# A graph network on one core: the order of the first loads, the block terms of edge places on GpSimd, and the block-end sums on ScalarE

## The chip, the cores and the metric

One core of one Trainium2 chip. A core has five instruction queues that run beside each other and wait for one another through semaphores: TensorE (PE, with its weight loads shown as PEld), VectorE (DVE), ScalarE (ACT), GpSimd (POOL) and SyncE (SP), which here only issues DMAs. Each queue runs its instructions in order. The metric is the device time of one execution in microseconds; lower is better.

## The reference

Four graph layers run one after the other on 3125 nodes with 128 features and 100,000 edges. Each takes `relu(layernorm(x))` and adds its result to x.

```python
h = relu(layernorm(x)); x = x + L0(h)   # two graph attention layers, 4 heads, softmax over a node's incoming edges
h = relu(layernorm(x)); x = x + L1(h)   # Lanczos steps: w = segment_sum(edge_weight * v[src], dst), three times, then 4 products
h = relu(layernorm(x)); x = x + L2(h)   # three mean-aggregating layers: segment_sum(h[src], dst) / degree, two products each
h = relu(layernorm(x)); x = x + L3(h)   # relu(msg_W @ [x[src], type embedding]) summed by dst, a product, layer norm
```

The edges come sorted by destination. `edge_weight` and `edge_type_16` are one number each per edge.

## The kernel before

Nodes are cut into 25 blocks of 128 (`NB`, `P`). The kernel turns the edge list into dense 128 x 128 adjacency blocks once and then works with matrix products. The stages that matter here are these.

*Places* (`place_edges`). Edges are laid out as 112 rows of 896 (`A`, `EC`). Raw fields arrive by DMA: `raw_dst`, `raw_edge_weight` and `raw_dst_next` on SP's queue, `raw_src` and `raw_edge_type` on ScalarE's. VectorE computes the destination block `db`, the source block `sb` and its pair, then counts in 13 masked sums (L989) what an edge row carries over to the next one (`carry`, L998). ScalarE splits the weights into three bf16 parts and copies transposed fields into `rec`. Then, in two parts (`HALVES`: 512 and 384 of the 896 columns), VectorE computes for each edge

- block terms that depend only on `db` and `sb`: `cap`, how many slots the block has, and `base`, where they begin (L1037 to L1048);
- its rank among the edges of the same pair of blocks, in 13 rounds of mask, scan and predicated copy (L1053 to L1056);
- from both, the place: lane, level, and an index into a table (L1060 to L1088).

GpSimd scatters the records into that table in DRAM with 782 indirect DMAs (L1096), one for each 128 edges, in the order `ORDER`, which begins at the edges of block 5. The table is filled with -1 before (`none`, L961). VectorE then tests that the edges of each block end where the program expects (`ENDS`, `LOW`): 25 compare-and-sum passes over `db` (L1107), a matrix product that sums over rows, and two small compares for each block (L1115, L1117). The result goes into `bad`, which decides at the very end whether a general version has to run instead.

*Layer 0's preparation* (`graph_and_layer0`): layer norm of x, projections, attention factors, and three bf16 parts of the scaled features (L1229 to L1328). x itself is loaded on SP's queue at the very start (L114, L115), since its DMA waits for nothing.

*Blocks and attention.* For groups of blocks (5 to 8, 9 to 12, ..., 21 to 24, then 0 to 2 and 3 to 4), `build_block` loads the block's slots from the table (L1167), which waits for all scatters that can hold its edges, turns keys with TensorE (L1173), makes one-hot matrices on VectorE (L1190, L1192), and multiplies them into the block's counts and weights (L1204, L1207). `attend` then runs the group's attention (L1365, L1379). Slots and keys have one buffer each, so the slots of a block are loaded while the block ahead of it is built.

A scheduler of the programming layer fixes the order of each queue at build time from program order, dependences and its own costs. A tile that is written again must first have been read by all its earlier readers; this holds across engines. The pool of `place_edges` is reused by layer 0's preparation.

Of the kernel before, what the change touches and what calls it, by code (L numbers as in the profile page):

```python
# [7 lines left out]
F32 = mybir.dt.float32  # L8
# [4 lines left out]
AF = mybir.ActivationFunctionType  # L13
OP = mybir.AluOpType
# [4 lines left out]
P = 128  # L19
N = 3125  # L20
NB = 25
# [30 lines left out]
EC = 896  # L52
# [848 lines left out]
class FastGnn(Gnn):  # L901
# [24 lines left out]
    def place_edges(self, placed):  # L926
# [9 lines left out]
        with ExitStack() as s:  # L936
# [14 lines left out]
            for name, dt, fill, skip, queue in loads:  # L951
# [2 lines left out]
                v = a[name[:3] if skip else name]  # L954
                queue.dma_start(t[:whole, :], v[skip : skip + whole * EC].rearrange("(p c) -> p c", c=EC))
                queue.dma_start(t[whole:, : rest - skip], v[whole * EC + skip :][None, :])
            nc.gpsimd.memset(rec, 0.0)
            per = BASE[NB] // P
            none = work.tile([P, 14 * ROOM], BF16, name="none")
            nc.gpsimd.memset(none, -1.0)  # L960
            nc.sync.dma_start(self.table[: BASE[NB]].rearrange("(p i r) f -> p i (r f)", p=P, r=14),  # L961
                              bc(none[:, None, :], [P, per // 14, 14 * ROOM]))
            number = tile("number")
# [31 lines left out]
            ps = psum.tile([P, P], F32, name="ps_small")  # L995
            nc.tensor.matmul(ps[:A, :n_pair], lhsT=before, rhs=tail, start=True, stop=True)
            carry = work.tile([A, n_pair], F32, name="carry")
            V.tensor_copy(carry, ps[:A, :n_pair])  # L998

            w = raw["edge_weight"]  # L1000
            parts = [tile(f"w16_{i}", BF16) for i in range(3)]
# [15 lines left out]
            for q, n in HALVES:  # L1017
                for f, t in fields:
                    ps = psum2.tile([P, 4, A], BF16, name="ps_rec")
                    for j in range(n):  # L1020
# [7 lines left out]
            names = (("cap", F32), ("base", F32), ("step", F32), ("rank", F32), ("r_i", I32), ("hi_i", I32), ("lane_f", F32),  # L1028
                     ("level_f", F32))
            t_cap, t_base, t_step, t_rank, t_r, t_hi, t_lane, t_level = (tile(m, dt) for m, dt in names)  # L1030
            idx = {}
            for i, (q0, n0) in enumerate(HALVES):
                lo, hi = q0 * P, (q0 + n0) * P
                cut = lambda t: t[:, lo:hi]

                cap, base, step, of_db = cut(t_cap), cut(t_base), cut(t_step), cut(db)
                V.tensor_scalar(cap, of_db, 24.0, 8.0, op0=OP.is_gt, op1=OP.mult)  # L1037
                V.tensor_scalar(cap, cap, 1.0, None, op0=OP.add)
                V.tensor_scalar(base, of_db, float(N_SLOTS[-1]), None, op0=OP.mult)
                for d in range(NB - 1):  # L1040
                    for _ in range(CAP[d] - CAP[d + 1]):
                        V.scalar_tensor_tensor(cap, of_db, d + 0.5, cap, op0=OP.is_lt, op1=OP.add)
                    more = N_SLOTS[d] - N_SLOTS[d + 1]
                    if more:
                        V.tensor_scalar(step, of_db, d + 1.0, float(more), op0=OP.min, op1=OP.mult)
                        V.tensor_add(base, base, step)
                V.tensor_tensor(step, cut(sb), cap, op=OP.mult)
                V.tensor_add(base, base, step)  # L1048
                rank = cut(t_rank)
                V.memset(rank, 1.0)  # L1050
                for b in range(n_pair):
                    mask = hot.tile([A, 4 * P], F32, name="mask4")[:, : hi - lo]
                    V.scalar_tensor_tensor(mask, cut(pair), float(b), cut(unit), op0=OP.is_equal, op1=OP.mult)  # L1053
                    run = hot.tile([A, 4 * P], F32, name="run4")[:, : hi - lo]
# [24 lines left out]
                nc.tensor.matmul(ps[:, :3], lhsT=self.ones[:A], rhs=wrong, start=True, stop=True)  # L1079
                V.tensor_reduce(self.bad[:, 2:3], ps[:, :3], axis=AX.X, op=OP.add)  # L1080
                V.copy_predicated(lane, bc(self.bad[:A, 2:3].bitcast(I32), [A, hi - lo]), cut(number))


                of = placed.tile([P, n0, A], I32, name=f"idx{i}")
                ps = psum2.tile([P, 4, A], F32, name="ps_idx")
                for j in range(n0):
                    nc.tensor.transpose(ps[:, j, :], t_lane[:, lo + j * P : lo + (j + 1) * P], self.ident[:A, :A])
                V.tensor_copy(of, ps[:, :n0])  # L1088
                for j in range(n0):
                    idx[q0 + j] = of[:, j]  # L1090
# [10 lines left out]
                self.placed[c] = st.ins  # L1101


            left = t_level
            sums = work.tile([A, NB], F32, name="sums")
            for d in range(NB):
                V.tensor_scalar(left, db, d + 0.5, None, op0=OP.is_lt, op1=OP.add, accum_out=sums[:, d : d + 1])  # L1107
            ps = psum.tile([P, P], F32, name="ps_small")
            nc.tensor.matmul(ps[:, :NB], lhsT=self.ones[:A], rhs=sums, start=True, stop=True)
            upto = work.tile([P, NB], F32, name="upto")  # L1110
            V.tensor_copy(upto, ps[:, :NB])
            beyond = work.tile([P, 2, NB], F32, name="beyond")
            V.memset(beyond, 0.0)
            for d in range(NB):
                V.tensor_scalar(beyond[:, 0, d : d + 1], upto[:, d : d + 1], float(ENDS[d] * P), None, op0=OP.is_gt)  # L1115
                if d:
                    V.tensor_scalar(beyond[:, 1, d : d + 1], upto[:, d - 1 : d], float(LOW[d] * P), None, op0=OP.is_lt)  # L1117
            V.tensor_reduce(self.bad[:, :1], beyond.rearrange("p i d -> p (i d)"), axis=AX.X, op=OP.add)


# [287 lines left out]
    def graph_and_layer0(self, counts, node):  # L1408
# [3 lines left out]
        with ExitStack() as s:  # L1412
            one = s.enter_context(tc.tile_pool(name="l0", bufs=1))
            self.open_attention(one)
            with ExitStack() as s2:
                tmp = s2.enter_context(tc.tile_pool(name="gat_h", bufs=1))
                two = s2.enter_context(tc.tile_pool(name="gat_r", bufs=2))
                psum = s2.enter_context(tc.tile_pool(name="gat_h_ps", bufs=3, space=PSUM))
                super().load_x()
                for i in (1, 2):  # L1420
                    self.attention_weights(tmp, i)
                for g in range(GN):
# [612 lines left out]
```

## Time and profile before

| | us |
|---|---|
| median of 3 runs | 3201.25 (3200.83 to 3203.47) |
| profiled execution, device time | 3195.56 |
| its span | 3193.8 |
| busy: PE, DVE, POOL, ACT | 2561.2, 2296.6, 1445.2, 917.4 |
| raw_dst lands, VectorE starts on it | 28.48 |
| first scatter (POOL L1096) | 108.30 |
| ends test starts, layer norm starts (DVE L1107, L1229) | 141.74, 174.97 |
| first one-hot of block 5 (DVE L1190) | 239.23 |

Times in the lower rows count from the start of the span. In a row of the timeline the first number is the start, the second the duration in us, then engine, line of the source, operation, output tile <- input tiles, shapes, count, and in brackets how long the engine sat idle before and what released it. "SPq" is a DMA issue on SP's queue; its duration is the time that the queue needed to issue it, not that of the transfer.

### The profile page before, as it was taken

What the parts mean: (1) busy time and instruction counts of PE and PEld (TensorE: products, weight loads), DVE (VectorE), ACT (ScalarE), POOL (GpSimd) and SP (SyncE); (2) the same over time, 40 slices, a digit from 0 to 9 for tenths busy, and PEclk for the clock granted to TensorE, in tenths of its full rate; (3) what the DMA queues carried; (4) which work ended last, traced back from release to release, by engine and by line L of the source; (5) the groups of instructions that cost most, each with busy time, mean ns of one, the idle gap of its engine ahead of it and who ended that gap; (6) DMA issues with size and microseconds to landing.
All of it is one profiled execution on the core that took longest, in us unless ns stands there. A gap on an engine that the chain in (4) does not pass through costs nothing. (4 is left out here: it accounts for less than half of the span.)

```text
span 3193.8 us, 52069 instructions
## 1 busy us (share of the span) xinstructions
PE 2561.2 (80%) x20788; PEld 1825.5 (57%) x20788; DVE 2296.6 (72%) x4015; ACT 917.4 (29%) x1785; POOL 1445.2 (45%) x1394
## 2 busy tenths in 40 slices
PE   0018787878787788798886999997999976989898
PEld 0017464646455655477675444445555546888897
DVE  7979999999989899899997010405455575666766
ACT  3035050505140212476665000002120212333333
POOL 1577777777777700055553000000120106777775
PEclk9979999999999999899999999998999997999999
DMA  6013130303131101000002878781000004444443
GB/s 187 14 18 98 25 98 20 98 20 101 31 94 28 51 32 62 1 2 1 1 1 80 298 272 302 273 301 45 1 1 1 5 18 138 130 139 133 128 131 85
DMA packets 127742, 276.54 MB, mean 87 GB/s; under 512 B 28645, under 2 KB 68468, under 8 KB 116532
## 3 DMA queue, kind: packets, MB, share of 16 engines
q1 hardware_dynamic: 62982, 198.30, 18.9%
q0 software_dynamic: 37856, 32.76, 4.8%
q10 hardware_dynamic: 26652, 42.05, 3.7%
q8 instruction: 165, 2.70, 0.4%
q14 instruction: 87, 0.71, 0.1%
HBM read 210.00 MB, written 63.02 MB: 85 GB/s over the span
## 5 line engine op out<-in xcount | busy, mean ns | idle before, releaser
L1096 POOL DMA_INDIRECT table<-rec,idx x782 | 773.6, 989 | 336.7 <-issue 237.4
L1365 DVE SCALAR_TENSOR_TENSOR over<-ps_row,minus,counts 128x512 bf16<-128x512 f32 (+3 forms) x1040 | 699.3, 748 | 15.9 <-ACT row L1483 12.0
L1379 PE MATMUL ps_acc<-parts,over 128*128 128x198 bf16 x5000 | 571.4, 251 | 134.1 <-POOL over L1362 34.7
L1379 PEld LDWEIGHTS <-over 128*128 128x128 bf16 x5000 | 391.8, 98 | 309.7 <-DVE over L1365 231.9
L1910 POOL DMA_INDIRECT m_far<-pre,src x401 | 397.8, 992 | 259.1 <-DVE skips L923 137.2
L1207 PE MATMUL ps_cw<-oh_w,oh_d 128*128 128x128 bf16 x4050 | 385.9, 224 | 56.7 <-DVE oh_w L1192 52.1
L1533 PE MATMUL ps_sum<-g,node 128*128 128x512 f32 (+1 forms) x1050 | 413.2, 552 | 12.9 <-DMA g<-weights 12.9
L1362 POOL TENSOR_TENSOR over<-above,counts 128x640 bf16<-128x640 bf16 x160 | 211.3, 1329 | 392.0 <-ACT above L1360 265.2
L1207 PEld LDWEIGHTS <-oh_d 128*128 128x128 bf16 x4050 | 303.8, 100 | 90.9 <-issue 68.7
L1204 PE MATMUL ps_cw<-oh_d,oh_s 128*128 128x128 bf16 x1350 | 299.0, 224 | 48.2 <-ACT w_out L1212 24.7
L1722 PE MATMUL ps_agg<-l_parts,counts 128*128 128x384 bf16 (+1 forms) x1875 | 317.3, 327 | 14.0 <-POOL l_parts L923 14.0
L1192 DVE TENSOR_TENSOR oh_w<-oh_s,keys 128x1024 bf16<-128x1024 bf16 (+2 forms) x561 | 325.4, 633 | 0.0
L1533 PEld LDWEIGHTS ps_sum<-g,node 128*128 128x128 f32 x1050 | 189.8, 192 | 222.1 <-issue 208.4
L1722 PEld LDWEIGHTS <-counts 128*128 128x128 fp8e4 x1875 | 183.5, 98 | 134.5 <-issue 11.3
L1754 POOL IOTA of_i<- 96x1 int32 x1 | 0.1, 135 | 480.2 <-PE ps_sum L1609 480.2
L1211 ACT ACTIVATE counts<-ps_cw 128x256 fp8e4<-128x256 f32 (+1 forms) x325 | 122.7, 378 | 303.9 <-PE ps_cw L1207 294.4
L1931 PE MATMUL agg_far<-m_far,oh_far 128*128 128x128 f32 x1246 | 173.8, 287 | 11.6 <-ACT m_far L1917 7.1
L1892 PE MATMUL agg_wide<-m_wide,oh_wide 128*128 128x128 f32 x1100 | 160.3, 289 | 26.5 <-ACT m_wide L1889 17.9
L1204 PEld LDWEIGHTS <-oh_s 128*128 128x128 bf16 x1350 | 133.6, 100 | 80.9 <-issue 49.9
L1347 PEld LDWEIGHTS <-counts 128*128 128x128 fp8e4 x1250 | 112.1, 98 | 102.3 <-ACT counts L1211 19.9
L1885 PE MATMUL ps_m<-skips,src_hot 128*128 128x128 bf16 x1650 | 159.3, 224 | 9.1 <-DVE src_hot L1875 9.1
L1931 PEld LDWEIGHTS agg_far<-m_far,oh_far 128*128 128x128 f32 x1246 | 156.6, 199 | 13.6 <-ACT m_far L1917 9.0
(353 smaller groups left out, 3532.1 us busy)
## 6 DMA issues: line engine op xcount, KB each, us to landing
g<-weights SPq DMA_DIRECT2D x75, 1024.0 KB
g<-weights SPq DMA_DIRECT2D x75, 576.0 KB
weights<-w_out ACTq DMA_DIRECT2D x150, 256.0 KB
src_row<-wide SPq DMA_DIRECT2D x32, 512.0 KB
table<-rec,idx POOLq DMA_INDIRECT x782
type_row<-wide SPq DMA_DIRECT2D x32, 384.0 KB
table<-none SPq DMA_DIRECT2D x1, 10864.0 KB
type_row<-types SPq DMA_DIRECT2D x25, 384.0 KB
```

The source lines that it names most:

```text
L1096: st = nc.gpsimd.indirect_dma_start(out=self.table, out_offset=bass.IndirectOffsetOnAxis(ap=idx[k][:, p : p + 1], axis=0), in_=rec[:, (k * ...
L1192: nc.vector.tensor_tensor(oh_w[:, t, :h], oh_s[:, :h], key(WT + t), op=OP.mult)
L1204: nc.tensor.matmul(ps[:, 0, j, :], lhsT=oh_s[of], rhs=oh_d[of], start=(j == c == 0), stop=last, skip_group_check=True)
L1207: nc.tensor.matmul(ps[:, 1, j, :], lhsT=oh_d[of], rhs=oh_w[:, t][of], start=False, stop=(last and t == 2), skip_group_check=True)
L1362: nc.gpsimd.tensor_tensor(over[:, : n * P], above, self.counts[:, sb, cols], op=OP.mult)
L1365: V.scalar_tensor_tensor(over[:, : n * P], row, minus[:, sb, i : i + 1], self.counts[:, sb, cols], op0=OP.is_gt, op1=OP.mult)
L1379: nc.tensor.matmul(banks[j // 2][:, j % 2, : 3 * F2], lhsT=over[:, j * P : (j + 1) * P], rhs=parts[:, sb, i].rearrange("p s f -> p (s f)") ...
L1533: nc.tensor.matmul(ps[:, c0 // 512, :m], lhsT=node[:, b, :], rhs=g[:, c0 - lo : c0 - lo + m], start=(b == 0), stop=(b == NB - 1))
L1722: nc.tensor.matmul(ps[:, :n], lhsT=self.counts[:, sb, db * P : (db + 1) * P], rhs=parts[:, sb, :n], start=(sb == 0), stop=(sb == NB - 1))
L1892: nc.tensor.matmul(agg, lhsT=oh[:, j, :], rhs=m[:, j, :], start=(x == 0), stop=(x == n_slots - 1))
L1910: nc.gpsimd.indirect_dma_start(out=m[:, j, :], out_offset=None, in_=pre, in_offset=bass.IndirectOffsetOnAxis(ap=src_of[:, a + j : a + j + ...
L1931: nc.tensor.matmul(agg[d], lhsT=oh[:, c - lo, :], rhs=m[:, c - a, :], start=(c == LOW[d]), stop=(c == ENDS[d] - 1))
```

## The change

There are three edits, and one reordering of two memsets.

- Loads: x is no longer loaded at the head of SP's queue but after the edge loads, the table fill and `types`; its DMAs also wait for the carry (`self.begun`). The memset of `none`, the source of the table fill, moves ahead of that of `rec`.
- Block terms: `cap` and `base` of both parts are computed on GpSimd ahead of the rank rounds. The fused compare-and-add of VectorE becomes a tensor_scalar and a tensor_tensor, 42 instructions in all, and a step of `CAP` by 4 is one pair instead of four fused ones.
- Ends test: ScalarE sums sign(2d + 1 - 2 db) over all edges for each block d, and VectorE compares the 25 sums with prepared limits in two instructions.

```diff
-            nc.gpsimd.memset(rec, 0.0)
             per = BASE[NB] // P
             none = work.tile([P, 14 * ROOM], BF16, name="none")
             nc.gpsimd.memset(none, -1.0)
+            nc.gpsimd.memset(rec, 0.0)
...
-            V.tensor_copy(carry, ps[:A, :n_pair])
+            self.begun = V.tensor_copy(carry, ps[:A, :n_pair]).ins
...
+            G = nc.gpsimd
+            for q0, n0 in HALVES:
+                cut = lambda t: t[:, q0 * P : (q0 + n0) * P]
+                cap, base, step, of_db = cut(t_cap), cut(t_base), cut(t_step), cut(db)
+                G.tensor_scalar(base, of_db, float(N_SLOTS[-1]), None, op0=OP.mult)
+                G.tensor_scalar(cap, of_db, 24.0, 8.0, op0=OP.is_gt, op1=OP.mult)
+                for d in range(NB - 1):
+                    more = N_SLOTS[d] - N_SLOTS[d + 1]
+                    if more:
+                        G.tensor_scalar(step, of_db, d + 1.0, float(more), op0=OP.min, op1=OP.mult)
+                        G.tensor_tensor(base, base, step, op=OP.add)
+                    if CAP[d] > CAP[d + 1]:
+                        G.tensor_scalar(step, of_db, d + 0.5, float(CAP[d] - CAP[d + 1]), op0=OP.is_lt, op1=OP.mult)
+                        G.tensor_tensor(cap, cap, step, op=OP.add)
+                G.tensor_scalar(cap, cap, 1.0, None, op0=OP.add)
+                G.tensor_tensor(step, cut(sb), cap, op=OP.mult)
+                G.tensor_tensor(base, base, step, op=OP.add)
...
-                V.tensor_scalar(cap, of_db, 24.0, 8.0, op0=OP.is_gt, op1=OP.mult)
-                V.tensor_scalar(cap, cap, 1.0, None, op0=OP.add)
-                V.tensor_scalar(base, of_db, float(N_SLOTS[-1]), None, op0=OP.mult)
-                for d in range(NB - 1):
-                    for _ in range(CAP[d] - CAP[d + 1]):
-                        V.scalar_tensor_tensor(cap, of_db, d + 0.5, cap, op0=OP.is_lt, op1=OP.add)
-                    more = N_SLOTS[d] - N_SLOTS[d + 1]
-                    if more:
-                        V.tensor_scalar(step, of_db, d + 1.0, float(more), op0=OP.min, op1=OP.mult)
-                        V.tensor_add(base, base, step)
-                V.tensor_tensor(step, cut(sb), cap, op=OP.mult)
-                V.tensor_add(base, base, step)
...
+            odd = work.tile([P, NB], F32, name="odd")
+            nc.gpsimd.iota(odd, pattern=[[2, NB]], base=1, channel_multiplier=0, allow_small_or_imprecise_dtypes=True)
+            limit = work.tile([P, 2, NB], F32, name="limit")
+            V.memset(limit[:, 1], -float(A * EC))
+            for d in range(NB):
+                V.memset(limit[:, 0, d : d + 1], float(2 * ENDS[d] * P - A * EC))
+                if d:
+                    V.memset(limit[:, 1, d - 1 : d], float(2 * LOW[d] * P - A * EC))
             sums = work.tile([A, NB], F32, name="sums")
             for d in range(NB):
-                V.tensor_scalar(left, db, d + 0.5, None, op0=OP.is_lt, op1=OP.add, accum_out=sums[:, d : d + 1])
+                nc.scalar.activation(t_level, db, AF.Sign, bias=odd[:A, d : d + 1], scale=-2.0, accum_out=sums[:, d : d + 1])
             ps = psum.tile([P, P], F32, name="ps_small")
             nc.tensor.matmul(ps[:, :NB], lhsT=self.ones[:A], rhs=sums, start=True, stop=True)
-            upto = work.tile([P, NB], F32, name="upto")
-            V.tensor_copy(upto, ps[:, :NB])
             beyond = work.tile([P, 2, NB], F32, name="beyond")
-            V.memset(beyond, 0.0)
-            for d in range(NB):
-                V.tensor_scalar(beyond[:, 0, d : d + 1], upto[:, d : d + 1], float(ENDS[d] * P), None, op0=OP.is_gt)
-                if d:
-                    V.tensor_scalar(beyond[:, 1, d : d + 1], upto[:, d - 1 : d], float(LOW[d] * P), None, op0=OP.is_lt)
+            V.tensor_tensor(beyond[:, 0], ps[:, :NB], limit[:, 0], op=OP.is_gt)
+            V.tensor_tensor(beyond[:, 1], ps[:, :NB], limit[:, 1], op=OP.is_lt)
...
-                super().load_x()
+                nc.vector.memset(self.x[:, NB - 1, :], 0.0)
+                x = self.a["x"]
+                for ld in (nc.sync.dma_start(self.x[:, : NB - 1, :], x[: (NB - 1) * P, :].rearrange("(b p) f -> p b f", p=P)),
+                           nc.sync.dma_start(self.x[:TAIL, NB - 1, :], x[(NB - 1) * P :, :])):
+                    self.wait_for(ld.ins, self.begun)
```

In the changed kernel's line numbers, the carry copy is L999, the rank rounds are L1059 to L1062, the Sign sums L1120, the two compares L1124 and L1125, and the scatter L1102. The tile `level_f` (`t_level`), which the sums use as their unread output, is also the tile in which VectorE forms the level of each place.

More of the change, by code (lines that the diff above doesn't have):

```diff
@@ L1034, in place_edges @@
                 cut = lambda t: t[:, lo:hi]
-                cap, base, step, of_db = cut(t_cap), cut(t_base), cut(t_step), cut(db)
-                V.tensor_scalar(cap, of_db, 24.0, 8.0, op0=OP.is_gt, op1=OP.mult)
-                V.tensor_scalar(cap, cap, 1.0, None, op0=OP.add)
-                V.tensor_scalar(base, of_db, float(N_SLOTS[-1]), None, op0=OP.mult)
-                for d in range(NB - 1):
-                    for _ in range(CAP[d] - CAP[d + 1]):
-                        V.scalar_tensor_tensor(cap, of_db, d + 0.5, cap, op0=OP.is_lt, op1=OP.add)
-                    more = N_SLOTS[d] - N_SLOTS[d + 1]
-                    if more:
-                        V.tensor_scalar(step, of_db, d + 1.0, float(more), op0=OP.min, op1=OP.mult)
-                        V.tensor_add(base, base, step)
-                V.tensor_tensor(step, cut(sb), cap, op=OP.mult)
-                V.tensor_add(base, base, step)
+                cap, base = cut(t_cap), cut(t_base)
                 rank = cut(t_rank)
@@ L1101, in place_edges @@
                 self.placed[c] = st.ins
-            left = t_level
+            odd = work.tile([P, NB], F32, name="odd")
[6 more added lines that the diff above has]
+                    V.memset(limit[:, 1, d - 1 : d], float(2 * LOW[d] * P - A * EC))
             sums = work.tile([A, NB], F32, name="sums")
             for d in range(NB):
-                V.tensor_scalar(left, db, d + 0.5, None, op0=OP.is_lt, op1=OP.add, accum_out=sums[:, d : d + 1])
+                nc.scalar.activation(t_level, db, AF.Sign, bias=odd[:A, d : d + 1], scale=-2.0, accum_out=sums[:, d : d + 1])
             ps = psum.tile([P, P], F32, name="ps_small")
             nc.tensor.matmul(ps[:, :NB], lhsT=self.ones[:A], rhs=sums, start=True, stop=True)
-            upto = work.tile([P, NB], F32, name="upto")
-            V.tensor_copy(upto, ps[:, :NB])
             beyond = work.tile([P, 2, NB], F32, name="beyond")
-            V.memset(beyond, 0.0)
-            for d in range(NB):
-                V.tensor_scalar(beyond[:, 0, d : d + 1], upto[:, d : d + 1], float(ENDS[d] * P), None, op0=OP.is_gt)
-                if d:
-                    V.tensor_scalar(beyond[:, 1, d : d + 1], upto[:, d - 1 : d], float(LOW[d] * P), None, op0=OP.is_lt)
+            V.tensor_tensor(beyond[:, 0], ps[:, :NB], limit[:, 0], op=OP.is_gt)
+            V.tensor_tensor(beyond[:, 1], ps[:, :NB], limit[:, 1], op=OP.is_lt)
             V.tensor_reduce(self.bad[:, :1], beyond.rearrange("p i d -> p (i d)"), axis=AX.X, op=OP.add)
```

## The prediction

> **What bounds the kernel now.** I read the page's engine rows first, then the waits, then the first 300 us in order of time, then busy time by stretch. The part that the change touches runs up to the first adjacency block, and beyond it the waits tell who passes a shift on.
>
> ```profile
> span 3193.8 us, 52069 instructions
> PE 2561.2 (80%) x20788; PEld 1825.5 (57%) x20788; DVE 2296.6 (72%) x4015; ACT 917.4 (29%) x1785; POOL 1445.2 (45%) x1394
> 51.80:108.30 56.50, 5.71 (x36) 3.90 (x36) 54.81 (x95) 20.01 (x25) 0.00 (x0) 1.00 0.21 66
> 141.70:175.00 33.30, 4.58 (x19) 3.42 (x19) 31.59 (x105) 3.30 (x4) 25.38 (x27) 1.00 0.11 31
> 233.00:1262.00 1029.00, 822.07 (x8558) 589.51 (x8558) 964.59 (x1678) 287.89 (x732) 675.74 (x694) 0.96 0.19 58
> ```
>
> The last three rows are stretches: length, then busy us of PE, PEld, DVE, ACT, POOL, then clock, DMA share, GB/s. VectorE is full while places are computed (54.81 of 56.50), full during the ends test, and 94% busy from 233 to 1262 us (blocks and layer 0's first attention). It is the bound from 28.5 us to 1262 us, so what moves its start there moves the end, unless the scatter becomes the later one. GpSimd is empty until the first scatter.
>
> ```profile
> 12.00:13.00 1.00, 0.00 (x0) 0.00 (x0) 0.00 (x0) 0.00 (x0) 0.00 (x0) 1.00 0.19 66
> ...
> 2.89 10.23 SPq L115 DMA_DIRECT2D x<-in_x_dram  x1
> 13.17 3.35 SPq L955 DMA_DIRECT2D raw_dst<-in_dst_dram  x1
> ...
> 28.48 0.63 DVE L968 TENSOR_SCALAR db_i<-raw_dst 112x896 int32<-112x896 int32 x1 [18.75 <-DMA raw_dst<-in_dst_dram]
> 35.08 1.09 DVE L921 TENSOR_TENSOR rest<-raw_edge_weight,w 112x896 f32<-112x896 f32 x1
> 108.30 1.26 POOL L1096 DMA_INDIRECT table<-rec,idx  x1 [98.65 <-DVE cap L1042]
> 141.74 1.08 DVE L1107 TENSOR_SCALAR_CACHE_REDUCE level_f<-db 112x896 f32<-112x896 f32 x1
> 291.43 0.27 SPq L1167 DMA_DIRECT2D slots<-table  x1
> 301.65 0.69 DVE L1190 TENSOR_TENSOR oh_s<-lane,keys 128x1024 bf16<-128x1024 bf16 x1 [1.32 <-PE keys L1173]
> ```
>
> Here x sits on SP's queue ahead of raw_dst, which VectorE awaits for 18.75 us. From 12 us the edge loads run at a DMA share of 0.19, three of 16 engines, about 70 GB/s. The last two rows belong to block 8: its slots are requested at 291.43, used at 301.65.
>
> **The change, part by part.** Zero is the start of the span.
>
> *Loads.* Moving x behind removes it from those three engines. ScalarE sees raw_dst, raw_edge_weight and raw_dst_next at 28.42, 33.55 and 38.82, so one 388.5 KB load alone takes about 5.2 us. First bytes move at 3 us. raw_src (ACT queue) and raw_dst (SP queue) will then share the three engines: 3 + 2 x 5.2, landing near 14.5. Type and weight share next, weight near 25, raw_dst_next near 30. VectorE starts 14 us earlier, but its seventh full-width step, L921, needs the weights and their ScalarE cast (0.94): 26.1 instead of 35.1. Gain: 9.0. The table fill moves up with them (its `none` memset of 0.46 no longer waits behind `rec`'s 5.33), and ends near 62 on the same three engines; the first scatter is far later, so it costs nothing. x now waits on SP for the carry (L999), behind types, whose issue stood 30.76 us[...]. It lands near 70; its reader, L1229, comes at 170. What is queued behind it (src_of, dst_of, the weights) is wanted later still. So zero, with 100 us of cover.
>
> *Block terms off VectorE.* Per half: base and cap (2), the add of 1, seven compare-adds, four min-multiplies, four adds, two closing operations. By the distance between starts (0.34 and 0.60 for 512, 0.27 and 0.47 for 384 elements) that is 10.2 us for the first half and 7.9 for the second. One stall of 1.6 us at 53.9 (of_i, behind ScalarE) is covered by then, too.
>
> *The same on GpSimd.* 22 tensor_scalar and 20 tensor_tensor. The nearest tensor_tensor row is L921 on POOL, 640 f32 in 1.36 us undisturbed, 2.13 ns an element: 10 x (512 + 384) x 2.13 = 19 us. No tensor_scalar of GpSimd is in the trace. Bounds: a free one-stream instruction (memset of rec, 0.85 ns; iota of number, 1.08 ns an element), and the two-input rate 2.13. "GPSIMD Engine Reference" (Engine selection) of the Trainium skill puts one-input operations near line rate, so I take 1.06: 11 x 896 x 1.06 = 10 us; at 2.13 it is 21. Sum 29 us (28 to 40). GpSimd starts when db is ready, near 17.5, and would be done long before the 108 us of its scatter. By busy shares this is free. A row speaks against it:
>
> ```profile
> 2281.76 2.18 POOL L1704 TENSOR_TENSOR skips<-skips,l_own 128x640 f32<-128x640 f32 x1 [24.94 <-DVE inv_col L1727]
> ...
> 2282.46 1.63 DVE L1730 SCALAR_TENSOR_TENSOR l_own<-agg_t,inv_col,l_own 128x128 f32<-128x128 f32 x1
> 2284.72 0.35 DVE L1730 SCALAR_TENSOR_TENSOR l_own<-agg_t,inv_col,l_own 128x128 f32<-128x128 f32 x1
> ```
>
> The same VectorE operation takes 0.35 alone and 1.63 while GpSimd adds 640 f32: it stood still for nearly all of GpSimd's 1.36. The Trainium skill says so as a rule ("SBUF — State Buffer", Who interferes with whom): the shared port pair is an exclusive lock, and a VectorE instruction with two SBUF inputs is fully blocked by a GpSimd one that reads SBUF; so is a one-input f32 one in a 2-port mode. Nearly all of VectorE's work here is such (masks, scans, predicated copies). So GpSimd's time is not beside VectorE's but inserted in it. By busy shares the sum below would end at -25; by row and rule, P is added to it. P is GpSimd's 29 us less what runs while VectorE waits anyway (17.5 to 26.1, less 3.4 us of its own work, about 6): P = 23, between 17 and 33.
>
> *Ends test.* Gone: 25 sums of 1.13 us on L1107, then 49 small compares; 174.97 - 141.74 = 33.2 us, with some idx work between. New: 25 Sign activations, whose output tile level_f is still read by VectorE's last lane step (start 140.65), so they can't start before it, though their input is ready at 17. Each: a cast of 896 took 0.94, Sign with a bias tile took 0.82 for 640 against 0.74 for a plain activation, and an accumulator read adds about 0.09: 1.16 with the wait. 25 x 1.16, four in_order copies that stand between (3.1), start 0.7, matmul and compares 1.4: 34.2 us. VectorE's queue holds L1124 ahead of the layer norm, so it waits. From 140.65 to 174.97 were 34.3. Worth nothing either way, between -3 and +4. The 50 memsets of `limit` (0.06 each) come before any load has landed.
>
> *Sums.* First scatter: -9.0 - 10.2 - 1.6 + 1.8 (more of the second half's rounds stand before it) + P = 4 us later, at 112. VectorE's norm: -9.0 - 18.1 - 1.6 + P = 6 us earlier. So the scatter is what is late next. Block 8 needs the first 133 scatters; the 133rd issues at 289.0, its slots load at 291.43, and 4.7 us from load to transposes (233.13 to 237.84 for block 5) make 296.1; the transposes stand at 301.1. Slack 5.0. Scatters slowed to 1.85 us while VectorE scans become fewer, 1 us back. The end then moves by the later of VectorE (-6) and scatter (4 - 1 - 5 = -2): about 4 us of VectorE's gain goes into a new wait for the slots of block 8. In general, end = P - 25. Later blocks have tens of us of slack (block 9's slots come 65 us before use), and the chain after 1262 us is unchanged, so it passes on one to one.
>
> The profiled execution took 3195.56 (span 3193.8), 5.7 below the median 3201.25. I apply the shift of -2 to the median: 3199.
>
> **Rivals.**
> A. The lock costs less than the row says: GpSimd fits between VectorE's instructions, P near 0 to 15. For it: VectorE did not slow when scatters ran beside its scans, GpSimd did (1.54 against 0.97). Against it: the row above. End -10 to -25, 3176 to 3191.
> B. Slower: GpSimd's tensor_scalar at the two-input rate or with more overhead, P of 31 or more. Place: masks and first scans, then the first scatter at 121 or later, and VectorE waiting at block 8. It decides from P = 31.4, where P - 25 passes 6.4 us (0.2%). At 2.13 ns P is about 32, +7; with 0.15 us more for each of 42 operations, +13: 3208 to 3214. For it: two-operation compares are not plain streams. Against it: the memset and iota rates.
> C. The loads do not come early: queues issue in another order and weights land at 29. Then +3 on either.
>
> **How the numbers follow.** 0.2% is about what a measurement of this kernel tells from no change, 6.4 us. Main case (P 18 to 31), 0.45: -7 to +6, of which 0.12 faster, 0.28 same, 0.05 slower. A, 0.27: 0.26 faster, 0.01 same. B with C, 0.28: 0.25 slower, 0.03 same. Faster 0.38, same 0.32, slower 0.30. The main case's own range is 3194 to 3207; with both signs likely, the range reaches to most of A and B: 3179 to 3212.
>
> **What would show it.** Right: raw_dst landing near 14.5, L921 near 26; L989 masks of 1.09 stretched to about 1.6 to 2.1 while GpSimd works; first scatter at 110 to 115; VectorE idle some 34 us ahead of L1124; a wait for PE keys of several us before block 8. Wrong: masks at 1.09 with the first scatter near 90 (A); GpSimd's tensor_scalar above 1 us for 512 elements and the first scatter beyond 120 (B); Sign activations that start before the last lane step.

## The result, and the profile after

| | before | changed |
|---|---|---|
| median on the same chip, 20 runs each, us | 3201.25 (3195.09 to 3208.02) | 3208.19 (3200.32 to 3214.38) |
| ratio, 95% interval | 1 | 1.0017 (1.001 to 1.0023) |
| span of the profiled execution, us | 3193.8 | 3206.5 |
| VectorE's L921; first scatter | 35.08; 108.30 | 23.74; 112.20 |
| layer norm of x starts | 174.97 | 167.41 |
| 159th scatter done (the last that block 9 needs) | 323.1 | 324.3 |
| first one-hot of block 9 | 392.99 | 394.61 |

The ratio of 1.0017 is 5.4 us (the medians lie 6.9 us apart): a small loss where I had forecast a gain of 2. The page of the changed kernel begins:

```profile
span 3206.5 us, 52074 instructions
PE 2568.5 (80%) x20788; PEld 1831.3 (57%) x20788; DVE 2275.1 (71%) x3926; ACT 943.4 (29%) x1835; POOL 1516.8 (47%) x1437
```

VectorE has 21.5 us less to do, GpSimd 71.6 and ScalarE 26 more. The same stretches as before:

```profile
51.80:112.20 60.40, 4.81 (x31) 3.23 (x28) 60.32 (x68) 14.77 (x20) 44.16 (x28) 1.00 0.14 40
134.90:167.40 32.50, 4.79 (x20) 3.34 (x20) 2.00 (x7) 30.44 (x54) 24.68 (x26) 1.00 0.11 31
225.00:1263.00 1038.00, 823.80 (x8557) 592.22 (x8557) 964.44 (x1676) 287.54 (x732) 676.09 (x702) 0.95 0.19 57
3.00:8.00 5.00, 0.00 (x0) 0.00 (x0) 5.00 (x4) 0.00 (x0) 5.00 (x3) 1.00 0.19 69
8.00:12.00 4.00, 0.00 (x0) 0.00 (x0) 1.71 (x4) 0.00 (x0) 1.62 (x2) 1.00 0.20 80
12.00:13.00 1.00, 0.00 (x0) 0.00 (x0) 0.63 (x1) 0.90 (x1) 0.00 (x0) 1.00 0.90 316
```

Until the first scatter VectorE is as full as before, with fewer instructions, and GpSimd is busy beside it. During the ends test ScalarE is full and VectorE empty. The edge loads come first: from 3 to 12 us they run at a share of 0.19 to 0.20, no faster than before, only earlier. In the 0.90 of 12 to 13 us the table fill is running beside them. In order of time:

```profile
1.72 0.25 SPq L955 DMA_DIRECT2D raw_dst<-in_dst_dram  x1
...
12.17 0.63 DVE L968 TENSOR_SCALAR db_i<-raw_dst 112x896 int32<-112x896 int32 x1 [2.47 <-DMA raw_dst<-in_dst_dram]
16.91 0.63 DVE L968 TENSOR_SCALAR sb_i<-raw_src 112x896 int32<-112x896 int32 x1 [4.12 <-DMA raw_src<-in_src_dram]
...
23.74 1.49 DVE L921 TENSOR_TENSOR rest<-raw_edge_weight,w 112x896 f32<-112x896 f32 x1
...
112.20 1.98 POOL L1102 DMA_INDIRECT table<-rec,idx  x1 [15.20 <-issue]
...
134.91 1.04 ACT L1120 ACTIVATE level_f<-db,odd 112x896 f32<-112x896 f32 x1 [39.74 <-DVE lane_f L1079]
...
166.70 0.18 DVE L1124 TENSOR_TENSOR beyond<-ps_small,limit 128x25 f32<-128x25 f32 x1 [29.20 <-PE ps_small L1122]
...
298.53 0.69 DVE L1198 TENSOR_TENSOR oh_s<-lane,keys 128x1024 bf16<-128x1024 bf16 x1 [6.69 <-PE keys L1181]
```

The last row is block 8, whose one-hots began at 301.65 before: 3.1 us earlier. Block 5 had been 8.5 us earlier (230.76 against 239.23); the rest went into block 8's wait of 6.69 us. At block 9 nothing of the gain is left. TensorE between 322 and 336 us, first before, then changed (a row is a run of like instructions):

```profile
326.24 2.00 PE L1379 MATMUL ps_acc<-parts,over 128*128 128x198 bf16 x20
328.71 0.48 PE L1173 MATMUL keys<-ident,slots 50*128 50x50 bf16 x5 [0.47 <-DMA slots<-table]
329.12 5.04 PE L1379 MATMUL ps_acc<-parts,over 128*128 128x198 bf16 x36
```

```profile
323.70 2.00 PE L1387 MATMUL ps_acc<-parts,over 128*128 128x198 bf16 x20
330.44 0.51 PE L1181 MATMUL keys<-ident,slots 50*128 50x50 bf16 x5 [4.74 <-DMA slots<-table]
330.89 5.31 PE L1387 MATMUL ps_acc<-parts,over 128*128 128x198 bf16 x34
```

The five transposes of block 9's keys stand in TensorE's queue between the 20th and the 21st of these products of the first group's attention (blocks 5 to 8). TensorE is at them 2.5 us earlier than before (325.70 against 328.24) and then waits 4.74 us for slots that were requested 1.7 us later (326.10 against 324.42), because the 159th scatter was done 1.2 us later. VectorE stands behind it: the row `over` at 331.76 was released by `ps_acc` after 4.00 idle us. So block 9's slots stop the attention of blocks 5 to 8, 65 us before VectorE uses them.

### The profile page after: what moved, and what is told of

It is laid out like the page before. It is cut to its first block, busy times and chain, and to the rows that moved or that the text cites. A ratio compares the mean times of both kernels' runs of the same rounds, so it can differ in the third digit from the quotient of the medians.

```text
span 3206.5 us, 52074 instructions
## 1 busy us (share of the span) xinstructions
PE 2568.5 (80%) x20788; PEld 1831.3 (57%) x20788; DVE 2275.1 (71%) x3926; ACT 943.4 (29%) x1835; POOL 1516.8 (47%) x1437
## 5 line engine op out<-in xcount | busy, mean ns | idle before, releaser
L1102 POOL DMA_INDIRECT table<-rec,idx x782 | 764.5, 978 | 253.3 <-issue 253.0
L1734 PEld LDWEIGHTS <-counts 128*128 128x128 fp8e4 x1875 | 183.6, 98 | 134.3 <-issue 11.3
## 6 DMA issues: line engine op xcount, KB each, us to landing
type_row<-wide SPq DMA_DIRECT2D x32, 384.0 KB
type_row<-types SPq DMA_DIRECT2D x25, 384.0 KB
```

What stands on the lines that cost most here:

```text
L1102: st = nc.gpsimd.indirect_dma_start(out=self.table, out_offset=bass.IndirectOffsetOnAxis(ap=idx[k][:, p : p + 1], axis=0), in_=rec[:, (k * ...
L1734: nc.tensor.matmul(ps[:, :n], lhsT=self.counts[:, sb, db * P : (db + 1) * P], rhs=parts[:, sb, :n], start=(sb == 0), stop=(sb == NB - 1))
```

## Experiments

Theory S: once the scatters are late, the time at which the last scatter of block 9 is done sets everything up to the end of the first attention. Rival V: VectorE's queue sets it, as the prediction assumed for all blocks behind the 8th. Rival L: the later stages, behind 1740 us, are slower in the changed kernel.

Two of the six sets of runs fell on chips where the kernel before itself takes 4355 to 4364 us instead of 3199 to 3203; there only the ratio, the first 180 us and the stages behind the scatters are read, and it is said at each of them.

### One part at a time

Loads alone: the hunks of `none`, `begun` and `load_x`.

> The kernel before with the loads part alone (edge loads and table fill ahead of x, x behind the carry). VectorE's L921 is then at 24 instead of 35.1 us, as in the changed kernel, and everything in the places stage 11 us earlier: first scatter near 97, layer norm near 164, the 159th scatter (the last that block 9 needs) done near 312 instead of 323.1. Theory S (the scatter path to block 9 sets the end of the opening): both scatter and VectorE come 11 us earlier, so 11 us less at the first block of the second group, about 3190. Rival V (VectorE's queue alone sets it, as my prediction had it for all blocks behind the 8th): the same 11 us. Rival L (the part of the changed kernel's loss that shows after 1740 us, some 4 us, is made by the loads): 3194.

Measured: 3192.66, ratio 0.9969 (0.9958 to 0.9981). L921 at 23.87, first scatter 97.1, norm 163.8, 159th scatter done 313.1, block 9's one-hots 383.5. Ten microseconds, as S and V both had it. L's 7 us is inside the interval (6 to 13), so by the time alone L could be in the loads.

Block terms alone: the hunks of `G`.

> The kernel before with the block terms on GpSimd alone. Before's loads, so L921 at 35.1. With the P of 24.7 us that the changed kernel shows, the first scatter comes at 112.3 + 11.3 = 123.6, the 159th is done at 324.4 + 11.3 = 335.7 (12.6 later than before), and the layer norm starts at 174.97 - 18.1 - 1.6 + 24.7, near 179 (4 later). Theory S: the wait for block 9's slots sets the end, 12 us later, 3213. Rival V: only VectorE's 4 us count, 3205. Rival L (terms make the loss after 1740 us): 4 more on either.

Measured: 3217.8, ratio 1.0047 (1.0034 to 1.006), 15 us. First scatter 124.4, norm 180.7 (5.7 later), 159th scatter 336.3 (13.2 later), one-hots 407.0 (14.0 later). S; V's 4 us, and 8 with L added, are outside the interval (11 to 19).

Sign sums alone.

> The kernel before with the Sign sums on ScalarE alone (in the tile that VectorE's last lane step reads). The sums start behind that step, near 141, and the layer norm near 174, about 1 us earlier than before; the scatters stay where they are. Theory S: 0. Rival V: -1. Rival L (the sums make the loss after 1740 us): +4, 3205.

Measured: 3201.91, ratio 0.9998 (0.999 to 1.0007). Norm 173.6. Block 9's one-hots are 3.3 us late in this one profile, because the scatters lost 2.7 us by the 11th (the third took 2.94 us, 1.32 before); the median doesn't show it. The sums are worth nothing, as forecast, and L's 4 us is outside the interval.

The undo in the changed kernel: all block terms back on VectorE, in the fused form that they had before.

```diff
-                G.tensor_scalar(base, of_db, float(N_SLOTS[-1]), None, op0=OP.mult)
...
+                V.tensor_scalar(base, of_db, float(N_SLOTS[-1]), None, op0=OP.mult)
...
```

> The changed kernel with the block terms back on VectorE, all else as in the changed kernel. First scatter near 97 (112 in the changed kernel), the 159th done near 311 to 314. Theory S: block 9's first one-hots near 382 to 384, 3190 to 3192, that is 13 to 17 us less than the changed kernel. Rival V: 5 us less than the changed kernel, 3203.

Measured: 3190.31, ratio to before 0.9971 (0.996 to 0.9982), against 3206.59 for the changed kernel beside it. First scatter 96.6, norm 162.1, 159th scatter 313.6, one-hots 384.0. S. Without this one move the change gains 9 us; with it, it loses 5 to 9.

### Ten scatters less

In both runs below the general version of the computation follows at the end, so their totals (13275 and 13262) are not comparable; the opening is read.

```diff
-            for c in ORDER:
+            for c in ORDER[10:]:
...
-        need = [self.placed[c] for c in range(LOW[db], ENDS[db])]
+        need = [self.placed[c] for c in range(LOW[db], ENDS[db]) if c in self.placed]
```

> The changed kernel without its first 10 scatters (1,280 edges stay unplaced; the scatters behind them start at the same time, all other work is the same). It tests whether the arrival of the slots of block 9 is what the changed kernel waits for. At 1.27 us a scatter the 159th of before's count is done 12.7 us earlier, near 312. Theory S: TensorE's waits for slots between 290 and 400 us (10.0 us in the changed kernel) go, VectorE's gain of 7.6 us comes through, and block 9's one-hots start near 386 instead of 394.6: 8 to 9 us less than the changed kernel, 3199. Rival V: the scatter is no bound behind block 8, at most the 3 us that block 8 waits: 3205 to 3208.

> The kernel before without its first 10 scatters, as a control for the run on the changed kernel. Here TensorE waits 0.5 us for slots between 290 and 400 us, so VectorE sets the end as much as the scatters do. Theory S: about 0.5 us less than before, 3201; a gain of 8 or more would say that later scatters, too, are waited for. Rival V: the same 0.

Measured in the changed kernel: TensorE's wait for slots, its largest between 290 and 400 us, is gone. From the waits (us in total, times, longest), the changed kernel first, then without the ten:

```profile
PE keys L1181 <- DMA slots<-table: 10.0, 2, 5.3
PE ps_acc L1387 <- DVE acc L1394: 2.5, 3, 0.8
PE ps_cw L1215 <- DVE oh_w L1200: 2.4, 2, 2.2
```

```profile
PE ps_cw L1215 <- DVE oh_w L1200: 4.5, 6, 2.2
PE ps_acc L1387 <- DVE acc L1394: 2.5, 3, 0.8
PE ps_cw L1212 <- ACT w_out L1220: 2.1, 5, 0.5
```

Block 9's one-hots start at 385.33 instead of 394.61, 9.3 us earlier; 386 was expected. That is 7.7 us ahead of the kernel before: VectorE's gain (7.6 at the norm) comes through as soon as the slots are there. In the kernel before the same cut brings nothing (393.1 against 392.99). There scatter and VectorE were level, with 0.5 us of waiting. So from the start there was no slack behind block 8, and the changed kernel made the scatters the later of two equals. S is shown in both directions; V fails.

### VectorE far ahead

Here the block terms are on VectorE and the sums have a tile of their own.

```diff
+            t_sign = tile("sign")
             for d in range(NB):
-                nc.scalar.activation(t_level, db, AF.Sign, bias=odd[:A, d : d + 1], scale=-2.0, accum_out=sums[:, d : d + 1])
+                nc.scalar.activation(t_sign, db, AF.Sign, bias=odd[:A, d : d + 1], scale=-2.0, accum_out=sums[:, d : d + 1])
```

> The changed kernel with the block terms back on VectorE and a tile of their own for the Sign sums' unread output. The sums can then start as soon as db is there and run on ScalarE beside the rank rounds, so that the layer norm starts right behind the last lane step, near 131 instead of 167. First scatter near 97, 159th done near 312. Theory S: the end moves with the scatter alone, 11 us less than before, 3190, although VectorE is 44 us ahead; VectorE then idles ahead of blocks 5 to 9. Rival V: up to 44 us less, 3157.

Measured: 3208.58, ratio 1.0017 (1.0008 to 1.0027). I had not seen that the freed sums would move ahead of ScalarE's other work. From the timelines of VectorE and of GpSimd:

```profile
51.87 0.63 DVE L968 TENSOR_SCALAR of_i<-raw_dst 112x896 int32<-112x896 int32 x1 [11.25 <-ACT field L1009]
```

```profile
113.49 1.26 POOL L1098 DMA_INDIRECT table<-rec,idx  x1 [103.70 <-DVE cap L1044]
```

Thirteen sums stand before ScalarE's field copy, for which VectorE's `of_i` waits; two waits for carries follow, and the first scatter is at 113.5, not 97. As a test it is the better for it: the norm starts at 158.0, 17 us earlier than before, and block 9's one-hots at 399.5, 6.5 us later, with the 159th scatter done at 328.1, 5 later. The time follows the scatter.

With each sum made to wait for the first half's indices (`first` is VectorE's copy into `idx0`):

```diff
+                self.wait_for(sg.ins, first)
```

> Loads part and Sign sums on ScalarE, block terms on VectorE; the sums have a tile of their own and wait for the first half's indices (near 96 us), so that they stand behind ScalarE's copies of fields and carries, not among them as in the run with early sums, where VectorE waited 11.25 us for of_i and 4.85 us for a carry. First scatter near 97 as with the loads alone, layer norm near 131. Theory S: the 159th scatter near 312 sets the end, so no more than the loads alone bring, 3191 to 3193, with VectorE idle ahead of each of blocks 5 to 9. Rival V: 33 us less than with the loads alone, 3160.

Measured: 3189.73, ratio 0.9976 (0.9966 to 0.9987). The norm starts at 140.4, the 159th scatter is done at 314.2, one-hots at 384.0. VectorE is 35 us ahead and gives all of it back. Its waits at the first one-hots of blocks 5 to 8:

```profile
221.84 0.69 DVE L1198 TENSOR_TENSOR oh_s<-lane,keys 128x1024 bf16<-128x1024 bf16 x1 [22.72 <-ACT wide_dl L1189]
242.94 0.69 DVE L1198 TENSOR_TENSOR oh_s<-lane,keys 128x1024 bf16<-128x1024 bf16 x1 [2.06 <-PE keys L1181]
263.73 0.69 DVE L1198 TENSOR_TENSOR oh_s<-lane,keys 128x1024 bf16<-128x1024 bf16 x1 [1.30 <-PE keys L1181]
288.04 0.69 DVE L1198 TENSOR_TENSOR oh_s<-lane,keys 128x1024 bf16<-128x1024 bf16 x1 [4.82 <-PE keys L1181]
```

The 22.72 went to `wide_dl`, ScalarE's copy of block 5's keys, and 4.82 to block 8's keys, both behind slots. Blocks 6 and 7 wait no longer than in the kernel before (1.78 and 1.32), and TensorE finds their slots there; the expected waits at every block did not come. At block 9 it is TensorE that waits, 4.79 us. It is no better than the loads alone, which is S. The loads alone, this version and the undo beat both kernels; they lie 8 to 10 us under the one before.

The runs on the chips where the kernel before takes some 3200 us, by their profiles (us):

| kernel | norm | 159th scatter done | block 9's one-hots | difference of the last two |
|---|---|---|---|---|
| before, two profiles | 175.0, 174.6 | 323.1, 323.5 | 393.0, 392.9 | 69.9, 69.4 |
| changed, two profiles | 167.4, 167.9 | 324.3, 324.1 | 394.6, 395.2 | 70.3, 71.1 |
| loads alone | 163.8 | 313.1 | 383.5 | 70.4 |
| terms alone | 180.7 | 336.3 | 407.0 | 70.7 |
| sums alone | 173.6 | 326.4 | 396.2 | 69.8 |
| changed, terms back | 162.1 | 313.6 | 384.0 | 70.4 |
| early own sums | 158.0 | 328.1 | 399.5 | 71.4 |
| late own sums | 140.4 | 314.2 | 384.0 | 69.8 |

The last column moves by 2 us, while from norm to one-hots there are 218 to 244.

### An earlier first scatter

Halves of 3 and 4 columns of 128 instead of 4 and 3, on the version with late sums.

```diff
-HALVES = ((0, 4), (4, EK - 4))
+HALVES = ((0, 3), (3, EK - 3))
```

> The same, with the two halves cut as 3 and 4 columns of 128 instead of 4 and 3, so that the first scatter comes a quarter of a half earlier (near 88) and the second half's indices are there before the first 27 scatters are issued. Theory S: all scatters up to the 159th are some 8 us earlier (304), and since VectorE is far ahead, the end is too: 3184. Rival V: no change from the run with 4 and 3.

Measured: 3219.08, ratio 1.0062 (1.0049 to 1.0075): 20 us slower, against both theories. The scheduler put 77 scatters of the first half and then 103 of the second in a row, so block 5 needed the 104th (the 81st with 4 and 3) and its slots were requested at 250.7 instead of 216.2. An order written in the source holds only as far as the scheduler keeps it.

With the scatters behind the 27th made to wait for the second half's indices, so that the written order holds (on a 4355 us chip):

> The run with late Sign sums and halves of 3 and 4 columns, but with the scatters behind the 27th made to wait for the second half's indices, so that they are emitted in the written order (in the run without it the scheduler put 77 scatters of the first half and 103 of the second in a row, and block 9 needed the 168th, block 5 the 104th). First scatter near 90, block 9 needs the 159th again, done near 306 instead of 314. Theory S: VectorE is far ahead, so the end moves with the scatter: 6 to 9 us less than with 4 and 3 columns (3189.7), 3181 to 3184. Rival V: no gain over 4 and 3.

Measured: ratio 0.998 (0.9966 to 0.9993); the terms-back version, on the same chip, had 0.9964 (0.9952 to 0.9977). No gain, and S's 306 for the 159th scatter was missed: 312.4, against 311.0 in the terms-back version. The first scatter came at 90.8, but:

```profile
90.82 3.74 POOL L1101 DMA_INDIRECT table<-rec,idx  x1 [81.03 <-DVE cap L1044]
94.86 3.46 POOL L1101 DMA_INDIRECT table<-rec,idx  x1 [0.30 <-issue]
98.62 3.28 POOL L1101 DMA_INDIRECT table<-rec,idx  x1 [0.30 <-issue]
102.21 2.66 POOL L1101 DMA_INDIRECT table<-rec,idx  x1 [0.30 <-issue]
```

A scatter's issue, 0.97 us at 318 us beside VectorE's bf16 one-hots, takes 3.74 beside its f32 steps of 512, and the 11th scatter is at 115.9 here and at 116.2 in the terms-back version. What is started earlier into these steps is only stretched.

### The tile of the sums

The changed kernel with the same `t_sign`, nothing else.

> The changed kernel with a tile of its own for the Sign sums' unread output, nothing else. It tests my step that the ends test is worth nothing because the sums wait for VectorE's last lane step. The sums start when db is there; VectorE's compares no longer wait for them, so the layer norm starts right behind the second half's indices, near 136 instead of 167.4. The first scatter is at 112 as in the changed kernel, or up to 5 us later, since a few sums stand ahead of ScalarE's field copies. Theory S: the end moves with the 159th scatter alone: as the changed kernel or up to 5 us more, 3206 to 3212. Rival V: up to 31 us less, 3176.

Measured (on a 4364 us chip): 4390.6, ratio 1.0057 (1.0032 to 1.0082). Both theories missed; the first scatter is at 141.3, where the changed kernel has 112.1 on this chip.

```profile
85.17 1.04 ACT L1121 ACTIVATE sign<-db,odd 112x896 f32<-112x896 f32 x1 [47.48 <-POOL odd L1111]
```

```profile
89.49 0.63 DVE L968 TENSOR_SCALAR of_i<-raw_dst 112x896 int32<-112x896 int32 x1 [40.96 <-ACT field L1009]
```

The iota of `odd`, 0.16 us of work, stands on GpSimd's queue behind all but the last two block terms (84.97). ScalarE reaches the sums early and waits 47 us for it, its field copies wait behind them, and VectorE waits 41 us for `of_i`. In the changed kernel the shared tile `level_f` prevents just this by holding the sums back.

It also leaves VectorE idle from 48.5 to 89.5, so that GpSimd's terms are seen undisturbed:

```profile
54.26 1.92 POOL L1042 TENSOR_SCALAR step<-db 112x512 f32<-112x512 f32 x1
56.26 1.50 POOL L1045 TENSOR_SCALAR step<-db 112x384 f32<-112x384 f32 x1
57.73 1.26 POOL L1043 TENSOR_TENSOR base<-base,step 112x512 f32<-112x512 f32 x1
58.94 0.99 POOL L1046 TENSOR_TENSOR cap<-cap,step 112x384 f32<-112x384 f32 x1
```

### The same kernels again

> The changed kernel once more, for a second profile and a second set of times on another occasion. The opening's shift (block 9's first one-hots 1.6 us later than before) explains a third of the measured difference. Theory S with chance: the rest, some 4 us behind 1740 us in the one profile, belongs to that set of executions, and the ratio comes out at 1.0005 to 1.001. Rival L (the later stages are slower in this kernel): 1.0017 again, and the product with `g` and the last layer's stage as long as in the first profile (433 us from first to last `g` product, 1033 us from there to the end).

> The kernel before once more, for a second profile. Its first profile was 5.7 us below the median. Theory S with chance: the first 1740 us as in the first profile within 1 us, and the stages behind it 3 to 8 us longer than there (428 us from first to last `g` product, 1027 us from there to the end), which makes up the difference to the median. Rival L: they are as short as in the first profile.

Both on the 4364 us chip: changed 1.0007 (0.9992 to 1.0023); before a single time of 4353.18. From first to last `g` product 435 and 431 us.

> The changed kernel once more. Theory S with chance: block 9's first one-hots again near 394.6, that is 1.6 us later than before, and the ratio to before at 1.0005 to 1.001. Rival L (its later stages are slower): 1.0017 again, with 433 us from first to last `g` product and 1033 us from there to the end as in its first profile.

> The kernel before once more, against itself: how far a ratio strays from 1 when nothing is changed, and a second undisturbed profile. Theory S with chance: ratio within 0.0005 to 0.001 of 1, block 9's one-hots within 1 us of 393.0, stages behind 1740 us 3 to 8 us longer than in its first profile (428.2 from first to last `g` product, 1026.9 from there to the end). Rival L: they are as short as there.

> The changed kernel with the block terms back on VectorE, all else as in the changed kernel. What the 24.7 us of GpSimd insert into VectorE's rank rounds goes, and VectorE's own 18.1 to 19.7 us come back: first scatter near 97 instead of 112, layer norm near 162 instead of 167.4. Theory S: the end moves with the scatters, 11 us less than before and some 13 to 15 less than the changed kernel: 3190. Rival V: with VectorE alone, 5 us less than the changed kernel: 3203.

On the 4355 us chip: changed 1.0006 (0.9995 to 1.0018), before against itself 0.9995 (0.9977 to 1.0013), terms back 0.9964. So on both of these chips the changed kernel can't be told from the one before.

> The changed kernel once more. Theory S with chance: block 9's first one-hots within 1 us of 394.6, and a ratio of 1.0005 to 1.001. Rival L (its later stages are slower): 1.0017 again, and from the first `g` product to the end 5 us or more above the kernel before in the same call.

> The kernel before against itself. Theory S with chance: ratio within 0.001 of 1, block 9's first one-hots within 1 us of 393.0, 1458 to 1464 us from the first `g` product to the end (1455.1 in its first profile). Rival L: 1455 again.

On a 3200 us chip: changed 3206.59, ratio 1.0027 (1.0015 to 1.004), one-hots of block 9 at 395.2; before against itself 1.0003 (0.9994 to 1.0011), one-hots at 392.9. So block 9's delay is 1.6 and 2.3 us in two pairs of profiles, and the ratios say 5.4 and 8.6. The remaining 4 to 6 us come again, as L has it, and are not in the opening. In the other kernels on such chips, but for the sums alone, the shift at block 9 and the measured one agree within 2 us.

From the first `g` product to the end the profiles of the changed kernel have 1466 and 1459 us, those of before 1455 and 1454 (not the 1458 to 1464 expected), the terms-back and loads versions 1463 each. All engines run the same instructions there. What differs is the clock that TensorE was granted. From the first to the last `g` product, before and then changed:

```profile
1738.70:2166.90 428.20, 420.40 (x1123) 197.56 (x1123) 59.17 (x57) 21.51 (x39) 0.00 (x0) 0.99 0.82 285
1740.30:2173.40 433.10, 423.67 (x1122) 198.91 (x1123) 59.02 (x57) 21.43 (x39) 0.00 (x0) 0.98 0.81 281
```

TensorE is busy nearly throughout, and in the eleven profiles on such chips (without the two that leave out scatters) this stage goes by the clock: three at 0.99 (both of before, the late sums) take 428 us each, eight at 0.98 take 430 to 435, both of the changed kernel among them. One hundredth of 428 us is 4 us, by estimate the size that is missing. Whether the change lowers the clock is not shown: the profiles of before are of executions 6 and 9 us under its medians, and the loads alone and the undo have 0.98 too, without a surplus in their medians. So the cause of this part stays open. It goes when the terms go back: 16 us between the two versions, of which 11 show at block 9. Whether the terms alone have it can't be told (15 us against 14, with an interval from 11 to 19).

## Why the prediction was wrong

**Loads.** Right, and a little better: raw_dst at 12.2 (14.5), L921 11.3 us earlier (9.0). The table fill and x cost nothing. The fill does not keep to three engines, as I had it: from 30 to 45 us, with the edge loads landed, the DMA share is 1.02.

**Block terms on GpSimd.** The right P by luck, from wrong numbers that cancel. From L921 to the second half's last lane step it was 35.08 to 140.65, 105.6 us; without VectorE's 18.1 and the stall of 1.6 that is 85.9. Measured are 23.74 to 134.27, 110.5. So P = 24.7 us, where I had 23. But the GpSimd work is not 29 us. Undisturbed, a tensor_tensor of 512 takes 1.26 (2.5 ns an element; I took 2.13), and a tensor_scalar of two operations 1.92 (3.75 ns; I took 1.06 and allowed 2.13). With 0.99 and 1.50 for 384 and 1.50 for a one-operation step the 42 come to about 59 us, twice my sum. Near line rate, which I took for one-input operations from the Trainium skill ("GPSIMD Engine Reference", Engine selection), is not what this case shows. And the lock did not insert all of it into VectorE: in the changed kernel the 42 took 76 us beside VectorE, which lost 24.7. GpSimd lost 17. The rule of the full block ("SBUF — State Buffer", Who interferes with whom), applied one to one as I did, would have given 53 from the true 59 (less the same 6 of cover). The section also says that whoever issues first gets the shared pair of ports and the other one blocks; I had charged every block to VectorE, and here both lost. Nor did the 6 us of cover (5.2 by its own terms) come: GpSimd starts at 19.24, and from there on VectorE waits for nothing up to its last lane step. The mask groups show VectorE's side, before and after:

```profile
L989 DVE SCALAR_TENSOR_TENSOR mask<-ending,unit 112x896 f32<-112x896 f32 x13 | 13.2, 1088 | 0.0
```

```profile
L989 DVE SCALAR_TENSOR_TENSOR mask<-ending,unit 112x896 f32<-112x896 f32 x13 | 17.8, 1435 | 0.0
```

A third more in the mean, 1.44 us, where I had expected 1.6 to 2.1.

**Ends test.** Right: 25 sums 1.17 us apart (1.16), 33.1 us from lane step to norm (34.2). Worth 1 us, and shown to be worth nothing in time.

**Sums.** First scatter 112.2 (112). Norm 7.6 earlier (6). Block 8 3.1 earlier (2). The two shifts that I built on were right.

**The step that failed** is in the prediction's sums: "Later blocks have tens of us of slack (block 9's slots come 65 us before use) ... so it passes on one to one." I took VectorE's one-hots at 393 for the first use of block 9's slots. The first use is the transposes of its keys, at 328.7, in the middle of another group's products on an in-order queue; before, TensorE waited 0.47 us there. Slack was nil, not 65. With it the sum would have read: the scatter's shift of +4 at the start, less what VectorE's earlier end gives back (2.7 us measured by the 159th), so +1.2, and block 9 shows +1.6. VectorE's whole gain goes into the two waits for slots, 5.3 us of TensorE at block 8, which the prediction had, and 4.74 at block 9, which it had not. The run without ten scatters shows it by giving the gain back.

**The second part** of the error is the 4 to 6 us behind 1740 us. The prediction said "the chain after 1262 us is unchanged", which is true of its instructions. Of the 7.4 us between its -2 and the 5.4 measured, 3.6 arise up to block 9 and 3.8 here. In the profiles these stages ran at a lower granted clock; whether the change lowers it is not settled.

**Rivals.** A (little lock) fell with P. B (dearer GpSimd) came true in its cause, tensor_scalar at 1.9 us, and not in its mechanism: P stayed below 31 and the first scatter at 112, not 121. That the time fell on its 3208 to 3214 is chance. (By the prediction's own terms the two-input rate gives P = 34, not 32.) C did not occur.

## What to carry to other kernels

The slack of a transfer ends at the first instruction in any in-order queue that waits for it, which may stand in front of work that has nothing to do with it: search the trace for that instruction before counting the cover. An offload to an idle engine can slow the bound engine, as GpSimd did VectorE; here 18 us of VectorE's work became 76 us of GpSimd's and 25 of VectorE's, and sat on the path to the first scatter. When two chains are level, as scatter and VectorE were here, only what advances both (the loads: 10 us) moves the end.

## What the hardware showed beside that

The interference goes both ways. Beside VectorE's f32 steps of 384 and 512 elements most of the scatters' issues on GpSimd take 1.5 to 3.7 us, against 0.97 beside its bf16 one-hots at 318 us.

On two of the chips the kernel before takes 4355 to 4364 us. There all queues but GpSimd's crawl from some 180 us to the last scatter near 1180 (VectorE is busy for 52 us of the 750 from 430 on). The DMA rows of 300 to 1000 us (packets, MB, share of 16 engines), first on the chip of the profile before, then there, show far fewer instruction packets:

```profile
q8 instruction: 44, 0.72, 0.5%
q14 instruction: 24, 0.20, 0.1%
```

```profile
q8 instruction: 2, 0.03, 0.0%
q14 instruction: 5, 0.04, 0.0%
```

In that time engines are idle without a releaser that the profile names. That they wait for instructions which come late behind the scatters' transfers is a reading of these rows, not tested; fewer packets also follow from less progress.
